# Layer 1 of a graph network stack: TensorE's order set by hand between convolutions and LSTM, and the first bias as a map

## The chip, the cores and the metric

The kernel runs on one core of one Trainium2 chip. The metric is the device time of one execution in microseconds (us), as the core measures it. Most numbers below come from traces: one execution of each kernel recorded by the hardware profiler, with the span from the first to the last instruction. A span is some 2 us shorter than the device time of the same execution.

Engines are called as the profile calls them: PE is TensorE's matmul pipeline, PEld its loading of weights, DVE is VectorE, ACT ScalarE, POOL GpSimd, SP SyncE, which here only issues transfers. PEclk is the clock granted to TensorE, as a share of full speed. `L163` is line 163 of the kernel's text; the two kernels number their lines differently.

## The reference

The input `x` is 128 sequences of 64 tokens of 256 channels, all fp32. A stack of four graph layers, each with a residual, works on them. The change concerns layer 1 alone:

```python
h  = relu(layernorm(x1))                    # x1 = x + output of layer 0
v  = relu(adj @ h @ Wg0 + adj @ bg0)        # first graph convolution, bias inside the adjacency
u  = v @ Wg1 + bg1
h  = relu(adj @ u)                          # second graph convolution
for p in 1..4:                              # LSTM over windows of p tokens
    h[windows of p] = lstm(Wih[p], Whh[p], bih[p] + bhh[p], h)
x2 = x1 + h
```

Layer 0 is a graph convolution with two batch norms before it; layers 2 and 3 are masked attention after it.

## The kernel before

The tokens are cut into 16 chunks of 512. Layer 1 takes two chunks at a time, a "super-chunk", of which there are eight. Of the code only what the change and the argument touch is shown; cuts are marked.

```python
def add_tokens(dst, base, src, name):       # base + transpose(src): at_b, at_d in the profile
    for h in range(NJ // 2):
        ps = bank(f"at{h}_{name}")          # one of 8 PSUM banks
        ...                                 # 4 transposes of 128x128 by matmul with ident
        nc.vector.tensor_add(dst[:, 2*h:2*h+2, :], base[:, 2*h:2*h+2, :], ps...)

def convolutions(c, hT):                    # chunk c; result goes to hT, channels on partitions
    nc.sync.dma_start(xt, xr[c])
    ...                                     # y = batch norm of layer 0's output (DVE)
    add_tokens(xs[c], xt, ... y ..., f"b{c}")
    layernorm_relu(h, xs[c], f"b{c}")       # DVE statistics, POOL power, ACT normalisation
    for k, ps in enumerate(aggregate(h, adjt_bd, f"b{c}")):     # agg_b: 8 matmuls of 128x128
        nc.vector.tensor_copy(agg[:, k, :], ps)
    for m in range(KD):
        ps = bank(f"v1_{c}_{m}")
        nc.tensor.matmul(ps, bg0_sb[:, m*P:(m+1)*P], adjt4..., start=True, stop=False)   # bias
        for k in range(KD):
            nc.tensor.matmul(ps, wg0_sb[:, k, m*P:(m+1)*P], agg[:, k, :], ...)
        nc.scalar.activation(v[:, m, :], ps, AF.Relu)
    ...                                     # u = v @ wg1 + bg1 (DVE adds)
    for k, ps in enumerate(aggregate(u, adjt_il, f"c{c}")):     # agg_c
        nc.scalar.activation(hT[:, k, :], ps, AF.Relu)

for sc in range(NCH // SUP):
    for i in range(SUP):
        convolutions(sc*SUP + i, hT[:, :, i*CH:(i+1)*CH])
    for p in range(1, SKIP + 1):
        ...
            lstm(p, hT[...], per, ...)      # blocks of gates: matmuls, ACT gates, DVE cell
    for i in range(SUP):
        ...                                 # hn = reordered copy of hT (POOL)
        add_tokens(xs[c], xs[c], ... hn ..., f"d{c}")           # the residual
```

An fp32 matmul appears in the trace as two records; so `x16` for agg_b is eight matmuls. In the kernel before, a scheduler puts the instructions in order on every engine.

## Time and profile before

| | before |
|---|---|
| time, median of 3 runs | 2523.06 us (2521.32 to 2523.38) |
| span of the trace | 2518.0 us |
| PE busy | 2293.2 us, 91% |
| layer 1, first LSTM to layer 2's first matmul | 349.39 to 1899.91 us |
| its period, a super-chunk | 198.05 us, seven times |
| layers 2 and 3 | 1899.91 to 2518.0 us |

Four lines of the page of the kernel before. The first is PE's busy time, share and number of records. The second is the granted clock in 40 equal slices, in tenths of full speed (9 is 90% or more). The third is the chain of work that ended last, by engine. The fourth is a group of instructions: busy time and mean ns of one, then the idle time of PE just before them and what ended it.

```profile
PE 2293.2 (91%) x9181; PEld 1485.8 (59%) x9181; DVE 897.6 (36%) x1892; ACT 825.6 (33%) x1479; POOL 178.7 (7%) x226
...
PEclk9999899989999999999999999999998898899998
...
PE 78%; DVE 10%; POOL 4%; ACT 3%; issue 2%; DMA 2%; SPq 0%; POOLq 0%; ACTq 0%; DVEq 0%
...
L163 PE MATMUL agg_b<-adjt_bd,h 128*128 128x128 f32 x256 | 61.4, 431 | 85.3 <-ACT h L153 85.3
```

PE carries the chain, but 85.3 us of its idle time stand ahead of a single group, agg_b, whose matmuls take 431 ns on average. That is where the convolutions wait for their normalisation, twice per super-chunk. The prediction below shows one such place in order of time.

### The profile page before, as it was taken

Reading aid. Unit: us, or ns where it says so; the run is one execution under the profiler, and the core shown is the slowest. Engines: PE = TensorE matmul, PEld = TensorE weight load, DVE = VectorE, ACT = ScalarE, POOL = GpSimd, SP = SyncE. Lnnn points to the kernel's source line nnn. Section 1 sums busy time; section 2 is a strip of 40 time slices with the busy share of each in tenths; the row PEclk is TensorE's granted clock in tenths of the full one; section 3 lists DMA queues with packets and bytes.
Section 4 is the critical chain, followed back from the end, with each engine's and each line's share of the span. In section 5 each row is a group of like instructions: output and inputs, shape, how many; then the busy total and the mean of one; then the engine's idle time right before and its main releaser. Section 6 shows DMA issues by size and latency. Waiting matters only on the chain.

```text
span 2518.0 us, 22830 instructions
## 1 busy us (share of the span) xinstructions
PE 2293.2 (91%) x9181; PEld 1485.8 (59%) x9181; DVE 897.6 (36%) x1892; ACT 825.6 (33%) x1479; POOL 178.7 (7%) x226
## 2 busy tenths in 40 slices
PE   6989699989989989989989989998997999989996
PEld 3544255854754764764674575575575666666665
DVE  5644322222232232231232232233223555555554
ACT  4544232323323323323323333233333323333331
POOL 2100100000010010010000000000002111111110
PEclk9999899989999999999999999999998898899998
DMA  3100400000000000000000000000000000000000
GB/s 94 59 0 1 150 14 1 1 17 1 1 17 0 1 17 0 1 17 1 1 9 9 1 9 9 0 1 1 0 1 30 16 10 18 17 9 18 17 17 18
DMA packets 30122, 37.78 MB, mean 15 GB/s; under 512 B 1856, under 2 KB 27456, under 8 KB 30016
## 3 DMA queue, kind: packets, MB, share of 16 engines
q1 hardware_dynamic: 27600, 27.89, 3.5%
q0 software_dynamic: 2256, 8.40, 0.9%
q8 instruction: 72, 1.18, 0.2%
q14 instruction: 34, 0.28, 0.0%
q10 hardware_dynamic: 160, 0.03, 0.0%
HBM read 27.93 MB, written 8.39 MB: 14 GB/s over the span
## 4 chain that ended last, share of the span: by engine, by line
PE 78%; DVE 10%; POOL 4%; ACT 3%; issue 2%; DMA 2%; SPq 0%; POOLq 0%; ACTq 0%; DVEq 0%
PE g L345 31%; PE g L352 16%; PE z L250 4%; PE o L567 3%; PE z L234 3%; PE p_q L446 3%; PE agg_b L163 2%; PE v L438 2%; PE u L318 2%; PE v L309 2%; PE p_k L446 2%; DMA xt<-in_x_dram 2%; DVE at L462 2%; ACT h L153 1%; PE agg_c L163 1%
## 5 line engine op out<-in xcount | busy, mean ns | idle before, releaser
L345 PE MATMUL g<-hT,wih 128*128 128x256 f32 (+2 forms) x2496 | 818.7, 483 | 3.8 <-ACT gate L368 3.8
L345 PEld LDWEIGHTS g<-hT,wih 128*128 128x128 f32 x2496 | 468.2, 188 | 334.2 <-issue 192.5
L358 ACT ACTIVATE gate<-g,bias 128x256 f32<-128x256 f32 (+2 forms) x624 | 350.6, 562 | 747.9 <-PE g L352 616.8
L352 PE MATMUL g<-hs,whh 128*128 128x256 f32 (+2 forms) x1536 | 435.8, 437 | 0.0
L352 PEld LDWEIGHTS g<-hs,whh 128*128 128x128 f32 x1536 | 291.3, 190 | 132.2 <-issue 62.0
L362 DVE TENSOR_TENSOR cell<-cell,gate 128x256 f32<-128x256 f32 (+2 forms) x96 | 48.7, 508 | 466.6 <-ACT gate L358 466.6
L163 PE MATMUL agg_b<-adjt_bd,h 128*128 128x128 f32 x256 | 61.4, 431 | 85.3 <-ACT h L153 85.3
L392 POOL COPY hn<-hT 128x512 f32<-128x512 f32 x32 | 36.3, 1210 | 1335.7 <-DVE hT L374 1335.7
L367 DVE TENSOR_TENSOR cell<-gate,gate 128x512 f32<-128x512 f32 (+2 forms) x80 | 48.2, 602 | 224.0 <-ACT gate L358 224.0
L234 PE MATMUL z<-agg,w_sb 128*128 128x512 f32 x256 | 116.3, 608 | 8.1 <-DVE agg L227 6.9
L250 PE MATMUL z<-h,w_sb 128*128 128x512 f32 x256 | 111.6, 599 | 5.0 <-ACT h L245 5.0
L163 PEld LDWEIGHTS agg_b<-adjt_bd,h 128*128 128x128 f32 x256 | 57.3, 314 | 90.0 <-ACT h L153 89.6
L368 ACT ACTIVATE gate<-cell 128x256 f32<-128x256 f32 (+2 forms) x176 | 89.9, 511 | 50.0 <-DVE cell L367 41.0
L567 PE MATMUL o<-v,att 128*128 128x64 f32 x512 | 77.1, 322 | 26.5 <-ACT att L472 26.5
L374 DVE TENSOR_TENSOR hT<-gate,gate 128x512 f32<-128x512 f32 (+2 forms) x80 | 48.1, 601 | 127.2 <-PE g L345 100.5
L567 PEld LDWEIGHTS o<-v,att 128*128 128x128 f32 x512 | 74.7, 235 | 29.9 <-ACT att L472 29.8
L250 PEld LDWEIGHTS z<-h,w_sb 128*128 128x128 f32 x256 | 49.2, 193 | 67.4 <-issue 57.2
L234 PEld LDWEIGHTS z<-agg,w_sb 128*128 128x128 f32 x256 | 48.0, 193 | 66.2 <-issue 47.8
L531 DVE COPY k<-p_k 64x512 f32<-64x512 f32 x64 | 44.1, 689 | 102.9 <-PE p_k L446 102.5
L446 PE MATMUL p_q<-hT,w_sb 128*128 128x512 f32 x128 | 73.9, 708 | 2.3 <-DVE hT L175 2.3
L153 ACT ACTIVATE h<-xs,nmr_b,rstd_b 128x256 f32<-128x256 f32 x64 | 33.2, 588 | 127.0 <-DVE nmr_b L151 127.0
L371 DVE TENSOR_TENSOR hs<-gate,gate 128x256 f32<-128x256 f32 (+2 forms) x96 | 47.8, 497 | 72.8 <-ACT gate L368 44.6
(151 smaller groups left out, 2406.2 us busy)
## 6 DMA issues: line engine op xcount, KB each, us to landing
xt<-in_x_dram SPq DMA_DIRECT2D x32, 512.0 KB, 3.9
out_dram<-o SPq DMA_DIRECT2D x16, 512.0 KB, 2.9
wih<-in_wih_t_dram POOLq DMA_DIRECT2D x4, 1024.0 KB, 13.1
whh<-in_whh_t_dram POOLq DMA_DIRECT2D x3, 1024.0 KB, 17.9
w_sb<-in_w_dram SPq DMA_DIRECT2D x1, 768.0 KB, 4.4
wqkv_sb<-in_wqkv_dram SPq DMA_DIRECT2D x1, 768.0 KB, 4.4
w_sb<-in_w1t_dram POOLq DMA_DIRECT2D x1, 512.0 KB, 4.6
w_sb<-in_w2t_dram POOLq DMA_DIRECT2D x1, 512.0 KB, 5.7
```

The source lines that it names most:

```text
L153: nc.scalar.activation(dst[:, j, :], src[:, j, :], AF.Relu, bias=nmr[:, j : j + 1], scale=rstd[:, j : j + 1])
L163: nc.tensor.matmul(ps[:, j * P : (j + 1) * P], src[:, j, k * P : (k + 1) * P], mat, start=True, stop=True)
L234: nc.tensor.matmul(ps, w1_sb[:, k, m * P : (m + 1) * P], agg[:, k, :], start=(k == 0), stop=(k == KD - 1))
L250: nc.tensor.matmul(ps, w2_sb[:, k, m * P : (m + 1) * P], h1[:, k, :], start=(k == 0), stop=(k == KH - 1))
L309: nc.tensor.matmul(ps, wg0_sb[:, k, m * P : (m + 1) * P], agg[:, k, :], start=False, stop=(k == KD - 1))
L318: nc.tensor.matmul(ps[:, i, :], v[:, k, j * P : (j + 1) * P], wg1_sb[:, k, :], start=(k == 0), stop=(k == KD - 1))
L345: nc.tensor.matmul(banks[q][:, :n].rearrange("p (j w e) -> p j w e", w=nw, e=2), wi[:, k, o], hv[:, k, :, cols, :], start=(k == 0), stop=( ...
L352: nc.tensor.matmul(banks[q][:, :n], wh[:, k, o], hs[:, k, :n], start=False, stop=(k == KD - 1))
L358: nc.scalar.activation(g[q], banks[q][:, :n], AF.Tanh if q == 2 else AF.Sigmoid, bias=bs[:, q * KD + c : q * KD + c + 1])
L368: nc.scalar.activation(g[2], cell[c], AF.Tanh)
L446: nc.tensor.matmul(ps, w[:, k, m * P : (m + 1) * P], hT[:, k, :], start=(k == 0), stop=(k == KD - 1))
L567: nc.tensor.matmul(ps[:, i, f], att[:, j * HEADS + hd, :], v[:, j, f], start=True, stop=True)
```

## The change

The change does two things. First, PE's order in layer 1 is set by hand: convolutions and residuals become generators that yield after each unit of work, and each unit of the next super-chunk is placed behind a block of gates of the current LSTM, so that PE has other work while a unit's input is made. The other engines are still ordered by the scheduler. Second, the first bias leaves PE. Since relu(z + c1) = max(z, -c1) + c1, with c1 = adj @ bg0 the same for every sequence, DVE takes the maximum against a map of -c1 made once, and the added c1 moves on through Wg1 into the next bias, c2 = c1 @ Wg1 + bg1.

```diff
+        for m in range(KD):
+            ps = bank(f"c1_{m}")
+            nc.tensor.matmul(ps[:, :P], bg0_sb[:, m * P : (m + 1) * P], adjt_bd, start=True, stop=True)
+            nc.scalar.copy(c1[:, m, :], ps[:, :P])
+            nc.vector.tensor_scalar(nc1[:, m, :], ps[:, :P], -1.0, None, op0=OP.mult)
+        ...                                                    # c2 = c1 @ wg1 + bg1
             add_tokens(xs[c], xt, lambda k, j: y[:, k, j * P : (j + 1) * P], f"b{c}")
+            yield                                              # and after agg_b, v, u, agg_c
-                nc.tensor.matmul(ps, bg0_sb[:, m * P : (m + 1) * P],
-                                 adjt4.rearrange("p j n -> p (j n)"), start=True, stop=False)
-                nc.scalar.activation(v[:, m, :], ps, AF.Relu)
+                nc.vector.tensor_tensor(v[:, m, :].rearrange("p (j n) -> p j n", n=P),
+                                        ps.rearrange("p (j n) -> p j n", n=P),
+                                        nc1[:, m, None, :].to_broadcast([P, NJ, P]), OP.max)
-                                     bg1_sb[:, None, :].to_broadcast([P, 2, D]))
+                                     c2[:, None, :].to_broadcast([P, 2, D]))
...
+        RESIDUAL = (0, 0, 1, 2)          # behind which block of gates each unit is put
+        CONV = (3, 5, 6, 7, 8)           # at_b, agg_b, v, u, agg_c of the next pair's first chunk
+        NEXT = 6                         # the second chunk's, so many blocks later
+        with tc.manual_schedule(engines={mybir.EngineType.PE}):
+            ...
+                for n, _ in enumerate(lstms(sc, hT_now)):
+                    for u in todo.pop(n, ()):
+                        next(u)
```

## The prediction

> **What bounds the kernel now.** I read the page's totals and slices first, then the chain, then one period of layer 1 in order of time on TensorE, then the engine table for stretches of it.

> The page gives PE 91% of a 2518 us span; the chain that ended last is PE for 78%, two thirds of it layer 1's LSTM gates (L345 31%, L352 16%). Layer 1 runs from about 291 to 1895 us as eight "super-chunks" of two chunks each. LSTM starts at 349.39, 547.44, 745.49 ... 1735.74 us: a period of 198.05 us, seven times over. So I look at one period. These are its last LSTM blocks and the stretch up to the next LSTM, PE only (start, duration, instruction, then in brackets the idle time before it and what ended it):

> ```profile
> 895.63 3.62 PE L352 MATMUL g<-hs,whh 128*128 128x256 f32 x16
> 899.08 0.60 PE L187 MATMUL at_d<-ident,hn 128*128 128x128 f32 x4
> 899.52 1.04 PE L187 MATMUL at_b<-ident,y 128*128 128x128 f32 x8
> 901.99 1.83 PE L187 MATMUL at_d<-ident,hn 128*128 128x128 f32 x12 [1.43 <-POOL hn L392]
> 909.10 3.77 PE L163 MATMUL agg_b<-adjt_bd,h 128*128 128x128 f32 x16 [5.29 <-ACT h L153]
> 912.70 1.02 PE L306 MATMUL v<-adjt,bg_sb 128*128 128x512 f32 x2
> 913.56 1.88 PE L309 MATMUL v<-agg,wg_sb 128*128 128x512 f32 x4
> ...
> 929.37 3.87 PE L163 MATMUL agg_b<-adjt_bd,h 128*128 128x128 f32 x16 [4.93 <-ACT h L153]
> ...
> 941.77 2.10 PE L163 MATMUL agg_c<-adjt_il,u 128*128 128x128 f32 x16
> 943.71 1.45 PE L345 MATMUL g<-hT,wih 128*128 128x512 f32 x3
> ```

> The 153.4 us of LSTM before 899.08 have only 0.48 us of idle PE. The 44.6 us after it (residual of two chunks, convolutions of the next two) have 1.43 + 5.29 + 4.93 = 11.65 us: PE waits for a chain POOL copy, transpose, DVE add, batch-norm statistics, POOL power, ACT normalisation, with no other work in its queue. The same stretch by engine (length, then busy time of PE, PEld, DVE, ACT, POOL, then the granted clock):

> ```profile
> 805.00:899.00 94.00, 94.00 (x371) 69.72 (x370) 24.78 (x51) 32.28 (x67) 2.58 (x2) 1.00 0.00 1
> 899.00:909.00 10.00, 3.31 (x26) 2.52 (x24) 6.70 (x18) 1.44 (x4) 3.31 (x4) 0.83 0.16 52
> 909.00:913.00 4.00, 3.90 (x17) 3.80 (x18) 0.79 (x2) 1.52 (x4) 0.00 (x0) 0.56 0.01 4
> 913.00:922.00 9.00, 9.00 (x34) 5.65 (x33) 2.22 (x5) 1.20 (x2) 0.00 (x0) 1.00 0.00 0
> ```

> LSTM runs at clock 1.00 with PE never idle and DVE and ACT at 26% and 34%; the aggregation after a wait runs at 0.56. That is a second cost: the 16 matmuls of agg_b take 3.77 us, the 16 of the same form in agg_c 1.94 (2.10 with the last one's tail).

> [...]gaps of 5.29 and 4.93 us are each followed by some 4 us at about half clock, and the 1.43 us gap is not. [...] So a convolution unit put behind a gate block before its input is ready would stall the LSTM behind it; whether it is ready must be worked out.

> **The change, part by part.** I compared the two programs' orders per engine. The work before layer 1 and PE's order of layers 2 and 3 are the same. In layer 1 the new order on PE is: after block 2 and block 3 of p=1 a chunk's residual transposes (at_d), after block 4 at_b of the next super-chunk's first chunk, then agg_b, v, u, agg_c of it each behind an LSTM block, and the same six blocks later for its second chunk. The last eight or so blocks (p=4) stand alone.

> 1. *Idle time removed*, per period: 11.65 us.
> 2. *Cold clock removed*: (3.77 + 3.87) - 2 x 1.94 = 3.76 us per period.
> 3. *Bias matmuls (L306) removed*: in the page's 16 chunks these are 64 records; warm, two take 0.86 us in the chain, and a chunk has four, so 1.72 us per chunk, 3.44 per period. They are on PE's path, since PE is the path. In their place the Relu leaves ACT (597 ns each) for a DVE max against a broadcast map; other DVE operations of 128x512 that read PSUM take 689 ns (the add of u). DVE gains 4 x 0.69 = 2.8 us per period on an engine busy 52.5 of 198. c1, its negative and c2 are made once, while layer 1 waits for its weights (291 to 307 us), so they cost nothing.

> Sum: 11.65 + 3.76 + 3.44 = 18.85 us per period, times seven periods: 132 us. A period becomes 153.4 + 25.8 = 179.2 us.

> **Are the inputs ready?** The tightest is agg_b, two blocks after at_b. In the trace the first of h follows the end of the transposes by some 5.3 us, the fourth by 7.1. In the new ACT order three of the four normalisations have a gate or tanh of p=2 (0.69 and 0.63 us) between them, and the last hT product delays DVE by about 0.7, so about 10 us (estimate). The two p=2 blocks in between have 24 records of 0.43 us = 10.3, and they start about 0.9 us after the transposes' end, so it just fits, by 1 to 2 us. v has a block of 13.9 us ahead of it, u likewise; agg_c has 12 records of 0.30 = 3.6 us (2.8 for p=4) against a DVE add of 0.69. at_d has two blocks of 5.2 us against about 5 us of POOL copies (1.21 each) after the last hT.

> *What is lost.* The old scheduler put four k=0 matmuls first in each new p, to cover the tail in which the last hT is written:

> ```profile
> 805.96 6.21 PE L345 MATMUL g<-hT,wih 128*128 128x336 f32 x20
> 806.16 0.69 ACT L358 ACTIVATE gate<-g,bias 128x512 f32<-128x512 f32 x1 [1.03 <-PE g L352]
> 806.75 0.62 ACT L368 ACTIVATE gate<-cell 128x512 f32<-128x512 f32 x1
> 807.40 0.69 DVE L374 TENSOR_TENSOR hT<-gate,gate 128x512 f32<-128x512 f32 x1 [0.82 <-ACT gate L368]
> ```

> PE's old work ended at 806.12 and hT was complete at 808.09, 1.97 us later, while PE ran on. The new order takes k=0 and k=1 of a gate together, which covers only two records (0.6 us). In seven super-chunks the gap is filled by at_b (0.95 us + 0.86 of k=0 against 1.7) or u (3.54 us against 1.97): I allow 0.3 us each, 2 us in all. The last super-chunk has no convolutions to put there: about 0.5 + 1.4 + 1.5 = 3.5 us.

> *The first pair*, before the first LSTM (349.39): nothing hides it. Its x arrives only at 307.5. In the new order DVE adds both chunks' x before it normalises either. The longest landing of an x tile there is 21.6 us; if it is the second chunk's, it arrives near 313, some 5 us late for chunk 0. Adding the rest by the same durations: both statistics by 318, h by 320 to 324, agg_b twice by 326.4, v 2 x 3.44, u 2 x 3.54, agg_c 2 x 1.94, so LSTM at about 344: 5 us won, not the 16 that two alternating chunks would give.

> Total: 132 - 2 - 3.5 + 5 = 131.5 us. 2523 - 131.5 = about 2391 us.

> **The rivals.**
> *A wait in place of the old one.* If h or a gate bank comes late behind each unit, PE stalls in the LSTM: two agg_b per period, each 2 to 3 us late, would give back 14 x 2.5 = 35 us: 2426. For it: the thin 1 to 2 us margin of the first agg_b[...]. Against it: ACT and DVE are idle two thirds of the time, the second agg_b has two blocks of 9.4 us ahead of it, and the eight banks are returned quickly (the ACT gate starts 0.02 us after its matmuls).
> *The gaps close but the clock is no better*, the array being throttled for another cause than the gaps: 7 x 3.76 = 26 us less: 2417. Against it: 94 us of unbroken PE at 1.00.
> *A DVE or ACT bound* in the middle of the period: the units cluster in the first 14 of 22 blocks. Against it: even 52.5 + 2.8 us of DVE in those some 110 us is half.
> *Hidden anyway*: if the bias matmuls and gaps were off the path the time would stay at 2523. Against it: PE's own order carries the chain through all of them.
> *Better than I think*: if both x tiles land together, up to 11 us more: 2380.

> **Range and chances.** The 132 us are differences of measured durations on a path that is one engine; the uncertain terms are waits: from about 0 to 35 us lost, and 0 to 11 us won. I take 2391 with 2376 to 2413. Only a stall of 80 us would bring the gain under 2% (50 us), so faster 0.97.

> **What would show it right or wrong.** Right: LSTM starts about 179 us apart; PE idle under 2 us per period; the granted clock 1.00 through it; agg_b's 16 records near 1.9 us in seven of eight pairs; no L306; the max on DVE near 0.69 us; LSTM's first block near 344 us; PE's share about 95%. Wrong: idle ahead of agg_b or the gates that names ACT h or DVE, a clock under 0.95 in the periods, or layers 2 and 3 no longer some 623 us long.

## The result, and the profile after

| | before | after |
|---|---|---|
| time, median of 4 runs each | 2522.52 us (2521.32 to 2523.38) | 2368.54 us (2367.89 to 2370.33) |
| ratio | | 0.9391, 95% interval 0.9375 to 0.9407 |
| span of the trace | 2518.0 us | 2365.9 us |

Every ratio here is the mean time of one kernel's fast runs over the mean of the other's of the same rounds, so it is not quite the ratio of the medians. The change saves 6.1%. The prediction was 2391 us with 2376 to 2413: the direction and most of the mechanism came true, but the kernel is 22 us faster than I said and lies below my range.

The page of the changed kernel, the same three rows as before:

```profile
PE 2224.8 (94%) x9125; PEld 1444.3 (61%) x9125; DVE 916.4 (39%) x1927; ACT 805.9 (34%) x1449; POOL 177.0 (7%) x222
...
PEclk9999979999999999999999999999998999999898
...
PE 82%; DVE 8%; POOL 3%; ACT 2%; DMA 2%; issue 2%; SPq 0%; POOLq 0%; ACTq 0%; DVEq 0%
```

PE's share is 94% (I expected about 95%). The clock row has 9s from the first LSTM to layer 2, but it had all but one there before: a slice of some 60 us is too coarse to show the half clock. Here is the stretch at the seam of two super-chunks on PE in order of time (start, duration, instruction, records; a bracket would tell idle time):

```profile
875.24 10.46 PE L365 MATMUL g<-hT,wih 128*128 128x512 f32 x24
885.54 1.04 PE L183 MATMUL at_d<-ident,hn 128*128 128x128 f32 x8
...
897.60 1.04 PE L183 MATMUL at_b<-ident,y 128*128 128x128 f32 x8
898.47 11.28 PE L365 MATMUL g<-hT,wih 128*128 128x512 f32 x24
909.58 1.95 PE L159 MATMUL agg_b<-adjt_bd,h 128*128 128x128 f32 x16
...
925.44 3.60 PE L324 MATMUL v<-agg,wg_sb 128*128 128x512 f32 x8
```

No line carries a bracket. at_b, then two blocks of gates (`x24`), then agg_b in 1.95 us, the last record's tail included; next come gates, and v in 3.60 us for 8 records with no bias matmuls among them. The table of a whole period by engine (length, then busy time of PE, PEld, DVE, ACT, POOL, then the granted clock) says the same:

```profile
875.30:1052.60 177.30, 177.26 (x650) 114.72 (x649) 54.87 (x111) 60.03 (x112) 7.16 (x8) 1.00 0.02 6
```

PE is busy 177.26 of 177.30 us at clock 1.00. In the trace's clock records TensorE's clock stays full without a break for 1419.9 us, from 326.7 to 1746.6 us of the span, while before it fell to half twice in a period, for 6.83 and 3.41 us (6.83 both times at the first seam).

The last super-chunk has no convolutions to mix in. There, three waits are left:

```profile
1607.31 18.64 PE L365 MATMUL g<-hT,wih 128*128 128x512 f32 x40 [0.48 <-ACT gate L388]
...
1648.90 11.75 PE L365 MATMUL g<-hT,wih 128*128 128x336 f32 x38 [1.42 <-DVE hT L396]
...
1694.94 5.33 PE L365 MATMUL g<-hT,wih 128*128 128x256 f32 x22 [1.25 <-DVE hT L396]
```

And before the first LSTM nothing hides anything:

```profile
315.02 1.28 DVE L185 TENSOR_TENSOR xs<-xt,at_b 128x512 f32<-128x512 f32 x2 [5.37 <-DMA xt<-in_x_dram]
...
321.74 6.27 PE L159 MATMUL agg_b<-adjt_bd,h 128*128 128x128 f32 x32 [14.44 <-ACT h L149]
```

DVE waits for the second chunk's x until 315.02, and agg_b starts only at 321.74.

So where did 152.1 us of span go? In four parts, from the starts of the LSTMs and of layer 2 in the two traces:

| part | before | after | saved | predicted |
|---|---|---|---|---|
| start to first LSTM | 349.39 | 345.36 | 4.0 | 5 |
| first LSTM to layer 2 | 1550.5 | 1407.9 | 142.6 | 126.5 (132 - 2 - 3.5) |
| layers 2 and 3 | 618.1 | 612.6 | 5.5 | 0 |
| sum | 2518.0 | 2365.9 | 152.1 | 131.5 |

Layers 2 and 3 have the same instructions in both kernels, but not the same time. Their row of the engine table, before and after:

```profile
1899.90:2518.00 618.10, 543.60 (x3164) 395.89 (x3164) 330.37 (x692) 194.41 (x349) 78.61 (x93) 0.91 0.04 14
```

```profile
1753.20:2365.90 612.70, 538.41 (x3164) 390.54 (x3164) 330.26 (x692) 194.40 (x349) 78.71 (x93) 0.92 0.04 14
```

3164 records in both, DVE, ACT and POOL as busy as before, and PE busy 5.2 us less, at clock 0.92 instead of 0.91. Whether this belongs to the change is taken up in the last experiments.

### The profile page after: what moved, and what is told of

It reads as the page before. It is cut to its first block, busy times and chain, and to the rows that moved or that the text cites. A ratio compares the mean times of both kernels' runs of the same rounds, so it can differ in the third digit from the quotient of the medians.

```text
span 2365.9 us, 22692 instructions
## 1 busy us (share of the span) xinstructions
PE 2224.8 (94%) x9125; PEld 1444.3 (61%) x9125; DVE 916.4 (39%) x1927; ACT 805.9 (34%) x1449; POOL 177.0 (7%) x222
## 4 chain that ended last, share of the span: by engine, by line
PE 82%; DVE 8%; POOL 3%; ACT 2%; DMA 2%; issue 2%; SPq 0%; POOLq 0%; ACTq 0%; DVEq 0%
PE g L365 34%; PE g L372 18%; PE z L246 5%; PE p_q L504 3%; PE z L230 3%; PE o L625 3%; PE v L496 2%; PE u L336 2%; PE p_k L504 2%; PE v L324 2%; DMA xt<-in_x_dram 2%; DVE at L520 2%; PE s L599 1%; PE agg_b L159 1%; POOL s L512 1%
## 5 line engine op out<-in xcount | busy, mean ns | idle before, releaser
L499 ACT COPY v<-v 128x512 f32<-128x512 f32 x64 | 37.1, 580 | 109.0 <-PE v L496 109.0
L381 DVE TENSOR_TENSOR gate<-gate,gate 128x256 f32<-128x256 f32 (+2 forms) x96 | 47.7, 497 | 55.8 <-ACT gate L378 55.8
L504 PE MATMUL p_q<-hT,wqk_sb 128*128 128x512 f32 x128 | 59.4, 607 | 10.1 <-DVE hT L171 10.1
```

The lines of the kernel that those rows point to most:

```text
L381: nc.vector.tensor_mul(g[0], g[0], g[2])
L504: nc.tensor.matmul(ps, w[:, k, m * P : (m + 1) * P], hT[:, k, :], start=(k == 0), stop=(k == KD - 1))
```

## The experiments

Three questions are open: which of the two parts of the change saves what; whether the slow agg_b was slow by the clock, as I assumed; and why layers 2 and 3 are faster. The kernels below ran in batches, each batch on one chip beside runs of the kernel before. For the reader's use, this is what their traces show (first LSTM's start, mean of the seven periods, eighth LSTM to layer 2, layers 2 and 3; all us, read from PE's order of time, so up to 0.3 us from the chain's starts above). With the hand order the first period has no residuals to place (175.5 us in the changed kernel, 177.27 in the other six), and those of the seventh super-chunk stand in "last".

| kernel | first LSTM | period | last | layers 2, 3 | span |
|---|---|---|---|---|---|
| before | 349.2 | 198.1 | 163.9 | 618.1 | 2518.0 |
| map_only | 347.2 | 196.3 | 162.9 | 615.2 | 2499.4 |
| order_only | 349.5 | 180.4 | 168.6 | 606.8 | 2388.0 |
| after | 345.2 | 177.0 | 169.0 | 612.6 | 2365.9 |
| clustered | 347.3 | 199.2 | 168.2 | 614.7 | 2524.8 |
| clustered_warm | 344.8 | 196.6 | 168.8 | 612.9 | 2502.5 |
| one_block | 347.3 | 180.7 | 169.5 | 607.5 | 2388.9 |
| best | 334.0 | 176.7 | 167.4 | 616.0 | 2354.3 |
| best2 | 330.8 | 176.7 | 168.6 | 618.0 | 2354.3 |

### map_only: the bias map without the order

```diff
 before, with:
-                nc.tensor.matmul(ps, bg0_sb[...], adjt4..., start=True, stop=False)
-                nc.scalar.activation(v[:, m, :], ps, AF.Relu)
+                nc.vector.tensor_tensor(v[:, m, :]..., ps..., nc1[...], OP.max)
```

> The kernel before with its scheduler's own order and only the bias map (16 chunks x 4 records of 0.43 us of L306 gone, max on DVE). Theory A (what the prediction took): the bias matmuls are wholly on PE's path, 16 x 1.72 = 27.5 us less: 2495 us. Theory B: in this order the two bias records after agg_b cover the DVE copy of agg (0.69 us), and without them PE waits for that copy, so only about 1 us a chunk is won: 2506 us, with a new idle of about 0.7 us in front of v that names DVE agg. Both: gaps of about 5 us before agg_b stay, period 198.05 - 3.4 (A) or - 2 (B).

Measured: 2501.42 us (2501.28 to 2503.42), ratio 0.9925 [0.991, 0.994], between the two expectations. By the table above, the period shrinks by 1.8 us, not by 3.44. PE's order of time shows why:

```profile
902.95 3.98 PE L163 MATMUL agg_b<-adjt_bd,h 128*128 128x128 f32 x16 [5.29 <-ACT h L153]
906.72 4.04 PE L320 MATMUL v<-agg,wg_sb 128*128 128x512 f32 x8
...
925.92 4.68 PE L320 MATMUL v<-agg,wg_sb 128*128 128x512 f32 x8
```

The bias matmuls had stood between agg_b and v. Without them v follows at once, and runs partly in the half clock that the wait before agg_b left behind (the granted clock was 0.88 and 0.76 in the two stretches): its 8 records take 3.88 and 4.51 us to the next instruction, against 3.43 in the changed kernel. Taking the bias matmuls out of that stretch pulled v into it.

### order_only: the order without the bias map

```diff
 after, with the bias matmul and ACT's Relu put back, and bg1 in place of c2
```

> The changed kernel with the bias matmuls put back (Relu on ACT, no map). Theory A: with the units behind gate blocks nothing waits, so the bias costs its full 1.72 us a chunk: period 177.27 + 3.44 = 180.7 us, 16 x 1.72 = 27.5 us in all: 2396 us. Theory B: part of it is hidden also here: under 2385. Idle of PE within a period under 0.2 us in both.

Measured: 2393.75 us (2389.86 to 2397.17), ratio 0.9501 [0.9483, 0.9518], as theory A says. The bias matmuls stand in PE's order without a wait before them:

```profile
939.97 1.02 PE L314 MATMUL v<-adjt,bg_sb 128*128 128x512 f32 x2
```

The period is 3.4 us longer than that of the changed kernel: in a stretch with no waits the bias matmuls cost their full 3.44 us. So the map is worth 1.8 us per period on the old order and 3.4 on the new, and the order saves 17.7 us per period alone. The two parts help each other.

### clustered: the hand order with the convolutions left together

```diff
-        CONV = (3, 5, 6, 7, 8)
-        NEXT = 6
+        CONV = (21,) * 5        # all behind the last block of gates
+        NEXT = 0
```

> The changed kernel with hand order and map, but all ten convolution units of the next two chunks behind the last gate block (chunk by chunk), not spread over the blocks. Theory A (the spreading is what wins, by filling the waits): two gaps of about 5 us before agg_b are back with the half clock after them (10.5 + 3.7 us), and about 0.7 us each before v, u and agg_c, since this order has nothing to cover them (4.4 us): period about 196 us, 2368 + 7 x 18.6 = 2498 us. Theory B (the scheduler's order as such was bad, a hand order alone wins): below 2430.

Measured: 2522.54 us (2519.75 to 2526.54), ratio 1.0008 [0.9991, 1.0026]; my estimate of 2498 was missed. The hand order with the bias map, but without the spreading, gains nothing at all. In PE's order of time:

```profile
909.16 3.60 PE L159 MATMUL agg_b<-adjt_bd,h 128*128 128x128 f32 x16 [5.24 <-ACT h L149]
...
917.16 3.29 PE L336 MATMUL u<-wg_sb,v 128*128 128x256 f32 x14 [0.35 <-DVE v L326]
...
1007.07 11.75 PE L365 MATMUL g<-hT,wih 128*128 128x336 f32 x38 [1.42 <-DVE hT L396]
```

The old wait of 5.24 us is there. New ones are added that the scheduler's order did not have: 0.35 us for v and 0.34 for agg_c in each chunk, and 1.42 and 1.25 us where a new p begins, since PE no longer starts with four records that need only the first half of hT. They eat what the bias map and the spread residuals saved. So it is the placing behind the gates that pays, not the hand order as such.

### clustered_warm: the same with dummy matmuls in the wait

```diff
+            if c >= SUP:
+                ps = bank(f"warm_{c}")
+                for r in range(6):                  # 12 records, in the wait before agg_b
+                    nc.tensor.matmul(ps, wg0_sb[:, 0, :P], wih_sb[0][:, 0, :CH], start=True, stop=True)
```

The result is right; the dummies' bank is never read.

> As clustered, with six matmuls of 128x512 whose result nobody reads (6 x 0.86 = 5.2 us) between at_b and agg_b, where PE would wait for h. The idle goes but the wait's length stays. Theory A (the half clock is caused by the gaps): agg_b's 16 records take 1.8 us instead of 3.6, granted clock 1.00, about 3.7 us less per period than clustered, 26 us in all. Theory B (the clock falls for another reason): same time as clustered within 5 us and agg_b still near 3.6 us. In all four runs layers 2 and 3 have the same instructions; if their time depends on where the clock's drops fall, it will differ from 618 (before) and 612.6 us (after) by a few us without relation to the edit.

Measured: 2504.54 us (2500.01 to 2506.30), ratio 0.9933 [0.9917, 0.9949]: 18 us less than clustered in the medians, where I expected 26. The period falls by 2.7 us, not 3.7. PE's order of time, and the engine table of the agg_b stretch:

```profile
895.22 5.32 PE L321 MATMUL warm<-wih,wg_sb 128*128 128x512 f32 x12
900.63 2.86 PE L160 MATMUL agg_b<-adjt_bd,h 128*128 128x128 f32 x16
```

```profile
900.60:903.40 2.80, 2.77 (x17) 2.11 (x17) 0.69 (x1) 1.45 (x3) 0.00 (x0) 1.00 0.00 0
```

The dummies fill the wait, the clock is 1.00, and yet agg_b takes 2.86 us instead of 1.95. ACT is busy here: it makes the four tiles of h in 2.08 us, one after the other, and agg_b needs them in turn. From its start to v's, agg_b takes 2.74 us here (2.63 for the second chunk), against 3.60 and 3.70 in the kernel before and 1.78 in the changed one. Of the 3.74 us per period (start to start; 3.76 in the prediction) that I put down to the clock, 1.93 are the clock's (0.86 + 1.07, cold less warm) and 1.81 are the pace of ACT (0.96 + 0.85, warm less unhindered). Spreading removes both, so my sum held; my cause was half of it.

### one_block: agg_b one block after at_b instead of two

```diff
-        CONV = (3, 5, 6, 7, 8)
+        CONV = (3, 4, 6, 7, 8)
```

> The changed kernel with agg_b moved up to one LSTM block behind at_b (instead of two). In the trace of the changed kernel h's fourth tile is ready 8.6 us after the end of at_b, and one block of p=2 takes about 5.2 us, so in seven super-chunks the first chunk's agg_b should wait on ACT h for about 2.5 us before its first matmul and be paced by h inside it: 7 x 2.5 = 17 us, 2386 us; the second chunk's agg_b stays where it is with no wait. Granted clock stays at 1.00 in the periods[...]. This is the size of the margin that the chosen schedule has. Rival (the margin is much larger than worked out, h comes in time anyway): no wait, 2368 us. Rival (the gap brings the half clock back too): over 2400 us.

Measured: 2391.20 us (2388.90 to 2394.07), ratio 0.9454 [0.9436, 0.9472], 24.4 us over the changed kernel in the same batch (2366.78); I expected 17. PE's order of time, at two neighbouring seams:

```profile
916.98 0.41 PE L159 MATMUL agg_b<-adjt_bd,h 128*128 128x128 f32 x2
917.97 0.98 PE L159 MATMUL agg_b<-adjt_bd,h 128*128 128x128 f32 x4 [0.58 <-ACT h L149]
920.05 2.50 PE L159 MATMUL agg_b<-adjt_bd,h 128*128 128x128 f32 x10 [1.10 <-ACT h L149]
...
1099.26 0.98 PE L159 MATMUL agg_b<-adjt_bd,h 128*128 128x128 f32 x4 [0.58 <-ACT h L149]
1101.33 1.38 PE L159 MATMUL agg_b<-adjt_bd,h 128*128 128x128 f32 x10 [1.10 <-ACT h L149]
```

The two waits are the same both times, 0.58 and 1.10 us. From the first record of agg_b to the gates behind it, the later seam takes 4.28 us: 2.50 over the 1.78 of the changed kernel, just the stall that I worked out. The earlier one takes 5.36 us, because the clock fell to half, where I had expected it to stay full:

```profile
917.00:920.00 3.00, 1.37 (x7) 0.80 (x6) 1.16 (x2) 3.00 (x6) 0.00 (x0) 0.98 0.00 0
920.00:923.00 3.00, 2.95 (x11) 2.63 (x12) 1.33 (x3) 0.00 (x0) 0.00 (x0) 0.50 0.00 0
```

In the clock records this happens in five of the seven super-chunks, each time for 3.41 us. No single gap here is longer than 1.1 us; what precedes the half clock is a stretch of 3 us in which PE is busy 1.37. In these seven it went with where the stretch falls on the raster of 3.413 us that the clock records show (see shift_1): the step that held most of agg_b was 26 to 33% full of matmuls in the five, 39 and 44% in the two that were spared. This also says how tight the chosen placing is: in the changed kernel the last h is ready at 907.20 us and agg_b starts at 909.58, a margin of 2.4 us (I had said 1 to 2). One block less costs 24 us. The seven periods grow by 25.5 us together: 7 x 2.5 = 17.5 are the stall, and the rest, 1.6 us in each of the five, the half clock.

### after_again, before_again, before_c, before_d, after_c: repeats

The kernels unchanged.

> The changed kernel unaltered, as a repeat and as the base of this batch. Theory: of my error some 5 us came from layers 2 and 3, which took 618.1 us in the trace of before and 612.7 in that of after with the same instructions, because the steps of about 3.4 us on which the clock falls are met by chance; then this profile should show another length of that stretch, between about 606 and 619 us, and layer 1 to within 0.5 us of the first time. Rival: the change shortens layers 2 and 3 in some fixed way, then 612.7 again within 0.5 us. Total 2368 us plus or minus 3 either way.

> The kernel before unaltered, one look at its trace. By the theory of chance, layers 2 and 3 take some length between 606 and 619 us that differs from 618.1; by the rival theory 618.1 again within 0.5 us. Layer 1's period stays 198.05 us within 0.3.

> The kernel before once more, for the length of layers 2 and 3 (618.1 and 618.75 us in its first two traces; 612.7 and 609.5 in the two of the changed kernel; 606.8 to 616.0 in the variants). If the length is chance[...], before should also show lengths under 616 in some traces; if the changed kernel shortens it, before stays at 618 to 619.

> As before_c, a fourth look at the kernel before: chance says somewhere in 606 to 619 us for layers 2 and 3; a fixed effect says 618 to 619.

> A third look at the changed kernel: chance says somewhere in 606 to 619 us for layers 2 and 3; a fixed effect says 609 to 613. Layer 1 the same as before within 0.5 us: first LSTM about 345.5, eighth about 1584.6.

Measured: after_again 2366.78 us (2364.99 to 2370.52), ratio 0.9359 [0.9342, 0.9375]; single looks of 2522.97, 2523.26 and 2521.16 us for before and 2368.78 for after. Layers 2 and 3 took 618.7, 618.1 and 618.1 us in the three new traces of before, and 609.5 and 612.6 in the two of after. So it looks like neither plain chance (the traces of before repeat too well) nor a fixed gain of the change. But four traces are few: the other fast runs of before in these batches lie between 2510.27 and 2531.60 us, with a mean granted clock of 0.960 and 0.949, so before varies more than its traces show. In after_again's batch before's median is 2530.66 us, so the ratio of the changed kernel came out lower than the first time; one_block and best, of the same batch, are better compared with after_again. Layer 1 repeats: first LSTM of after at 345.7 and 346.1, eighth at 1584.8 and 1585.2 us.

### shift_1, shift_3, shift_6: the kernel before with layers 2 and 3 moved a little

```diff
+            for r in range(1):                      # 3, 6
+                nc.vector.tensor_scalar(wqkv_sb[:, 0, :D], wqkv_sb[:, 0, :D], 1.0, None, op0=OP.mult)
             wt = w2s.tile([P, 3 * KD, D], F32, name="wt")
```

In the clock records of all traces the clock falls to half and rises again on a raster (a grid of equal steps) of 3.413 us, always for whole steps of it but for the last, which the trace's end cuts. My theory was that the place of layer 2's start in this raster sets how many steps are slow.

> The kernel before, with one in-place multiplication by 1.0 of part of layer 2's weights on DVE, on which TensorE's first transposes of layer 2 wait: nothing but a delay of about 0.6 us (estimate: 0.42 us for a DVE operation of 128x256 plus 0.2 to be seen). In the clock records of all fourteen traces the granted clock changes on a raster of 3.413 us. Counted from the last raster point, layers 2 and 3 begin at 0.51 to 0.60 us in all four traces of before (length 618.1 to 618.7), at 0.57 in best2 (618.0), 1.08 in one_block (607.5), 1.76 in order_only (606.8), 2.37 to 3.05 in the three of after and clustered_warm (609.5 to 612.9). If that position sets the length, this kernel begins at about 1.15 and layers 2 and 3 take about 607 us: a delay of 0.6 us makes the kernel about 10 us FASTER, 2512 us. Rival (the length goes with the kernel or with chance): 618 to 619 us, total 2522.

> As shift_1 with three such multiplications, a delay of about 1.4 us: layers 2 and 3 begin at about 1.95 us after a raster point and should take 607 to 609 us, total about 2513 us. Rival: 618 to 619 us, total 2523.

> As shift_1 with six such multiplications, a delay of about 2.6 us: layers 2 and 3 begin at about 3.15 us after a raster point, near where after began (2.65 and 3.05, 612.6 us) and before map_only's (0.03, 615.2), so 612 to 616 us, total about 2520 us. Rival: 618 to 619 us, total 2525.

Measured: shift_1 2530.18 us, ratio 1.0034 [1.0009, 1.0059]; shift_3 2522.03 us, 0.9998 [0.9963, 1.0034]; shift_6 2518.24 us, 0.9991 [0.9965, 1.0016]. The theory falls: shift_1 became slower, not 10 us faster, and shift_3 did not gain; only shift_6 lies where it should, which after the other two counts as luck. In shift_1, layers 2 and 3 look like this:

```profile
1900.60:2526.00 625.40, 551.93 (x3164) 404.03 (x3164) 330.62 (x692) 194.25 (x349) 78.24 (x92) 0.90 0.04 14
```

The positions in those expectations were also read carelessly: the records' zero lies some 10.5 us before the span's, by up to half a microsecond differently in each trace. With that set right, and the time at half clock within layers 2 and 3 summed from the records:

| trace | start after a raster point | at half clock | layers 2, 3 |
|---|---|---|---|
| order_only | 2.45 | 81.2 | 606.8 |
| one_block | 1.38 | 85.3 | 607.5 |
| after_again | 2.65 | 87.3 | 609.5 |
| after, after_c | 3.27, 3.03 | 97.2, 97.2 | 612.6, 612.6 |
| clustered_warm | 2.76 | 97.5 | 612.9 |
| clustered | 1.16 | 102.7 | 614.7 |
| map_only | 0.40 | 103.2 | 615.2 |
| shift_6 | 3.15 | 103.8 | 615.8 |
| best | 2.97 | 104.0 | 616.0 |
| shift_3 | 2.16 | 109.3 | 617.9 |
| before (4 traces), best2 | 0.73 to 0.95, 0.99 | 109.4 to 113.6 | 618.0 to 618.7 |
| shift_1 | 1.50 | 127.0 | 625.3 |

The length of layers 2 and 3 rises with the time at half clock, by some 0.4 us for each us of it: (625.3 - 606.8) / (127.0 - 81.2). The start alone does not set it: 1.38 gave 607.5 and 1.50 gave 625.3. Moving the start by 0.6 to 2.3 us changes it, by 7.2 us up (shift_1) or 2.3 down (shift_6), though nothing else in layers 2 and 3 is changed. So 5.5 us of the 152.1 go with the shorter time at half clock in this trace (109.5 us before, 97.2 after).

### best and best2: what the changed kernel's trace still offers

```diff
 after, with:
+        xt1 = {}                                    # the first pair's x ahead of the weights
+        for c in range(2):
+            xt1[c] = l1.tile([P, NJ, D], F32, tag="xt", name=f"xt1_{c}", bufs=2)
+            nc.sync.dma_start(xt1[c], xr[c])
...                                                  # bg0, bg1, bih, bhh loaded at the program's start
+            pair = [convolutions(i, parts[i]) for i in range(SUP)]
+            for u in pair:
+                next(u)                             # at_b first
+            ...                                     # then c1, nc1, c2
+                    pairs = [(q, k) for q in gates for k in range(KD)]
+                    if not s and not c:
+                        pairs.sort(key=lambda qk: qk[1])        # k=0 of all gates, then k=1
```

> The changed kernel with what its trace shows still to be had: the x tiles of the first pair are loaded ahead of layer 1's weights, the bias vectors at the very start and the bias map made after the first pair's transposes, so that the first LSTM should start near 326 us instead of 345.4 (y ready at about 295, both x tiles by 297, h by 304, agg_b to 309, then v 7, u 7, agg_c 3.6 us); and in the first LSTM block of each p all k=0 matmuls come before the k=1 ones, which covers four records more of the hT tail and should take about 2.5 of the 3.15 us of waits out of the last super-chunk. Expected 2368.5 - 19 - 2.5 = about 2347 us. Rival: the x loads only change places with the weights and the first LSTM waits for wih instead: 2360 us or more.

Measured: 2352.53 us (2348.99 to 2356.38), ratio to before 0.9301 [0.9284, 0.9318]; in the same batch the changed kernel has 2366.78 us, so this is 14 us better and beats both. The k order does as expected: the three waits of the last super-chunk are 0.48, 0.21 and 0.33 us instead of 3.15 in all. The first LSTM starts at 334.0 us, not 326. A DVE line shows what holds it:

```profile
305.42 0.42 DVE L444 TENSOR_TENSOR c<-c,bg_sb 128x256 f32<-128x256 f32 x1 [3.66 <-PE c L442]
```

The addition that makes c2 stands in DVE's queue ahead of the statistics and waits 3.66 us for its matmuls, which wait for wg, landed at 303.3. best2 moves it behind agg_b, and gives one chunk's last residual copies to DVE:

```diff
 best, with:
+            for u in pair:
+                next(u)                             # agg_b, then c2
+                eng = nc.vector if c == NCH - 1 else nc.gpsimd
+                eng.tensor_copy(hn[:, k, :]..., hT[:, k, :]...)
```

> The version best with two waits taken out that its trace shows: the addition that makes c2 stood ahead of the statistics of the first pair in DVE's queue and held them for 3.66 us (its matmuls wait for wg, which landed at 303.3 us); it now comes after agg_b. And in the last super-chunk one of the two chunks' residual copies goes to DVE instead of POOL, against a wait of 3.75 us before the last transposes. Expected: first LSTM near 329.5 us instead of 334.0, the wait before the last transposes about 2 us; 2352.5 - 4.5 - 1.5 = 2346 us. Rival: DVE is held by something else in the queue (the first pair's x) and the first LSTM stays near 334, 2351 us.

Measured: 2355.66 us (2351.70 to 2356.69), ratio 0.9334 [0.9296, 0.9372] in another batch. The first LSTM came forward to 330.8 us (expected 329.5). The wait before the last transposes did not shrink: it is 4.12 us. POOL, in order of time:

```profile
1724.05 2.73 POOL L503 MEMSET at<- 128x512 f32 x3 [2.29 <-PE g L370]
1726.72 1.43 POOL L405 COPY hn<-hT 128x512 f32<-128x512 f32 x1
```

A clearing of layer 2's buffers, 2.73 us, had been put into POOL's queue ahead of the copy. And this trace has 618.0 us in layers 2 and 3, where best has 616.0; that ate the rest. best and best2 are not told apart by these runs. Either beats both kernels; best was 14 us under the changed one in the same batch.

## Why the prediction was right or wrong

**What bounds it, right.** PE's order carried the time, and closing its gaps cut the time. (The gates are 47 of the chain's 78%, three fifths rather than the prediction's two thirds.) Idle PE in a period fell from 12.1 us (11.65 and the LSTM's 0.48) to 0.04.

**Step 1, idle time, right but too small.** I summed the idle times as the trace prints them. Each wait here cost more than its bracket. The last instruction before a gap has its tail of 0.17 us counted as busy, which back-to-back work hides, and the transposes between the waits ran slowly (12 records of at_d in 1.83 us, 1.31 in the changed kernel): 0.52 + 2 x 0.17 = 0.86 us per period. u and agg_c behind the waits took 0.19 and 0.26 us more than they do now, and two at_b transposes that the scheduler had put among agg_c's took 0.12 more. The LSTM's wait of 0.48 us between p=1 and p=2, which I left in the 153.4, vanished because at_b now stands in it. Together 0.86 + 0.19 + 0.26 + 0.12 + 0.48 = 1.9 us. The period is 177.27 us (each but the first) instead of 179.2.

**Step 2, the cold clock, right in its sum, half wrong in its cause.** That the half clock comes from the gaps was my estimate from one trace (half clock behind gaps of 5.29 and 4.93 us, none behind 1.43). The half clock is only half of that cost (1.93 of 3.74 us), as clustered_warm shows: at full clock, agg_b behind the wait still loses some 1.8 us per period to ACT's pace. That the sum held is partly luck: 3.77 and 3.87 include the last record's tail and 1.94 does not, and agg_c's 1.94 was itself slower than agg_b is now (1.78). From start to start it is 3.60 + 3.70 - 2 x 1.94 = 3.42 by the prediction's yardstick and 3.74 in fact. Nor does the half clock wait for the end of the gap: in the trace of before it begins at 905.68 us, 1.9 us into the wait of 5.29 us, behind a step filled to 31%.

**Step 3, the bias matmuls, right.** order_only shows 3.4 us per period in the new order. That it would be 1.8 on the old one (map_only) I had not seen. The maximum on DVE takes 0.69 us in the changed kernel, as estimated, and DVE is busy 54.87 of a period's 177.30 us.

**The allowance of 2 us for new waits, wrong.** "I allow 0.3 us each": in seven super-chunks next to nothing waits. From 348.9 to 1735.0 us PE is busy 1382.5 of 1386.1 us, and 3.15 of the missing 3.6 are the last super-chunk's. With step 1's 13.5 us (7 x 1.93) this makes up the error in layer 1: 13.5 + 2 + 0.35 = 15.9 of 16.1 us. With the 5.5 us of layers 2 and 3, less the 1.0 that the first pair fell short, that is 20.4 of the 20.6 us by which the spans differ more than predicted.

**The last super-chunk, right.** 0.48 + 1.42 + 1.25 = 3.15 us of waits for the 3.5 predicted (its three terms add up to 3.4).

**The first pair, right within 2 us.** x landed at 315 (313 predicted), and the first LSTM started at 345.4 us (344).

**Are the inputs ready, right.** agg_b has a margin of 2.4 us. That a unit put behind a gate block too early holds up the gates behind it, which the prediction took for granted, is shown by one_block: with a block taken away, agg_b waits 0.58 and 1.10 us for ACT's h, and the stall is 2.50 us. The rival "a wait in place of the old one" is thereby out; it would have been true for a placing one block tighter.

**Layers 2 and 3, wrong.** I named a length other than the old one as a sign of error (623 us, counted from the end of layer 1's work near 1895; 618.1 from layer 2's first matmul) and gave no term for it. It moves between 606.8 and 625.3 us over these kernels with time at half clock. Here it was worth 5.5 us.

**The range failed** because all its width on the fast side was one rival about x. The terms were differences of printed durations, each slightly too small in the same direction, and seven periods multiply that. 2 us in a period of 198 is what was missed.

## What to carry to other kernels

When one engine waits at the same place in every round, put the unit that waits behind independent work long enough for its input, and work out the margin: here two blocks give 2.4 us to spare, and one block costs 24 us. The value of such a wait is best taken from start to start, against the same instructions in a stretch without waits; that catches tails, slow neighbours and half clock together. The cost on the waiting path was not additive here: the same bias matmuls were worth 1.8 us per period before and 3.4 after.
